# Last part of a four-layer graph network: three of a quad's four batches scaled by a diagonal product on TensorE and one on ScalarE, in place of two and two

## The chip, the cores and the metric

The kernel runs on one core of one Trainium2 chip. The metric is the device time in microseconds. The kernel before takes 3130.37 us, the median of three runs from 3129.48 to 3130.62; the profiled execution has a span of 3128.8 us.

## The reference

Four layers, each a graph operation on x (128 batches, 128 nodes, 256 features), added to x and layer-normalized over the features. The change lies in the end of the last layer. Cut to that part:

```python
x_in = agg.reshape(-1, d)                     # agg = A_hat @ x
h   = relu(batchnorm(x_in @ W1.T + b1, g1, be1))
out = h @ W2.T + b2
out = batchnorm(out, g2, be2)                 # per feature, over all batches and nodes
x   = layernorm(x + out)                      # per node, over the 256 features
```

The second batch norm is a scale and a shift for each of 256 features. They are known only when `h @ W2.T` has been computed for all batches. What remains then is: scale and shift every feature, add x, and normalize each row of 256. All values are float32.

## The kernel before

**Tiling.** The 128 batches go in 32 quads of four (`QB` = 4, `NQ` = 32). For each quad `outs[q]` holds `h @ W2.T` in SBUF with features on the partitions: two chunks of 128 features (`DC` = 2), each 128 partitions x 512 columns, 128 columns (nodes) to a batch. The layer's input x lies with nodes on the partitions: `x3s[q]`, 128 x 1024, 256 columns (features) to a batch. It is loaded from HBM by the SyncE queue into twelve buffers (`load_x3`, L1509), eleven of them ahead of the stage.

So each quad must be turned from features on partitions to nodes on partitions, and scaled and shifted on the way. There are two ways in the kernel, two batches each:

- *The ScalarE way* (batches 0 and 1): `halves` (L1349) scales and shifts in place with one activation for each chunk, where scale and shift are one value for each partition. TensorE then transposes each 128 x 128 block into the PSUM bank `pt[0]` (L1520). VectorE adds the bank to x in SBUF (L1537).
- *The diagonal way* (batches 2 and 3): TensorE multiplies the unscaled block by `diag2`, a diagonal matrix of the scales, which transposes and scales at once, into the bank `pt[1]` (L1528). The shift is added to x by GpSimd (L1525, with `shift_bc`, a row of shifts repeated over the partitions). One more product, of x with the identity, 512 columns wide, adds x into the same bank (L1530). The sum stays in PSUM, and statistics and normalization read it there.

**The row normalization.** `moments(q, half)` (L1533) takes the statistics of two batches on VectorE (two instructions of L1540 and two of L1542); its first half begins with the addition of L1537. ScalarE takes the root (`sd`, L1584). `coefficients(q)` (L1544) makes the factor and the offset of each row with two small VectorE operations (L1547, and L1548, which reads `mvs` and `rs`, both in SBUF, and writes `nm`). `apply(q)` (L1551) is four activations of 256 columns on ScalarE, one for each batch (L1560), from SBUF for batches 0 and 1 and from PSUM for batches 2 and 3. They write into `x3s[q]`, and GpSimd issues the output DMA of the quad (L1566). In the last quad VectorE does two of the four.

**Order.** This part stands under a manual schedule: each engine's queue has the order in which the code issues, and each engine works through its queue in order. The loop at L1571 issues in iteration q:

1. `moments(q, 0)` on VectorE;
2. `scaled(q + 1)` (L1513): ScalarE's `halves`, TensorE's transposes, GpSimd's shift addition, TensorE's diagonal products and identity product;
3. `coefficients(q - 1)` on VectorE and `apply(q - 1)` on ScalarE, with the output DMA on GpSimd;
4. `moments(q, 1)` on VectorE and the root on ScalarE.

So on ScalarE the order is: `halves` of q+1, four applies of q-1, root of q. On VectorE: first half of q, coefficients of q-1, second half of q. On GpSimd: addition of q+1, output DMA of q-1, so that the addition of q+1 stands behind the output DMA of q-2. On TensorE: all of q+1.

**PSUM.** There are eight banks, handed out in turn; a quad takes two. At the start one more is used to make `shift_bc` (L1523).

Of the kernel before, what the change touches and what calls it, by code (L numbers as in the profile page):

```python
# [11 lines left out]
AF = mybir.ActivationFunctionType  # L12
# [14 lines left out]
def gnn_stack(ctx: ExitStack, tc: tile.TileContext, x, adj, w_qv_t, a, w_out_t, src, dst,  # L27
# [14 lines left out]
    nc = tc.nc  # L42
    B, N, D = x.shape
    H, DH = a.shape
    E = src.shape[0]
    P = 128
# [3 lines left out]
    QB = 4  # L50
# [11 lines left out]
    def ctile(shape, name, dtype=F32, pool=const):  # L62
        return pool.tile(shape, dtype, tag=name, name=name)

    def ps(name):
        return psum.tile([P, 512], F32, tag="ps", name=name)
# [6 lines left out]
    ident = ctile([P, P], "ident")  # L73
# [8 lines left out]
    sc2, sh2 = ctile([P, DC], "sc2"), ctile([P, DC], "sh2")  # L82
# [46 lines left out]
    with ExitStack() as phase:  # L129
# [556 lines left out]
        def layer2(k, b, room=None):  # L686
# [84 lines left out]
            pos = [ps("po2").rearrange("p (t d) -> p t d", d=D) for _ in range(2)]  # L771
            yield
            scaled(0)
            v.p4()
            yield
            v.p3()
            po = mix(0)
            scaled(1)
            yield
            mv = norm(0, po)  # L780
# [102 lines left out]
        bias = ctile([P, D], "bias", pool=cst2)  # L883
# [435 lines left out]
    with ExitStack() as phase:  # L1319
# [25 lines left out]
        diag2 = ctile([P, DC, P], "diag2", pool=cst)  # L1345
        shift_bc = ctile([P, D], "shift_bc", pool=cst)
        wide = ctile([P, DC, P], "wide", pool=cst)

        def halves(q, o, ag):  # L1349
            nc.scalar.activation(ag[:, o, :2 * N], ag[:, o, :2 * N], AF.Identity, bias=sh2[:, o:o + 1],  # L1350
                                 scale=sc2[:, o:o + 1])

        def spread(o):
# [3 lines left out]
        with tc.manual_schedule(engines=None):  # L1357
# [112 lines left out]
            def norm_over(o):  # L1470
                batch_norm(st2, o, bn2, sc2, sh2, K3 + o)
                halves(0, o, outs[0])
                spread(o)
# [31 lines left out]
            x3s, sums, mvs, coefs = {}, {}, {}, {}  # L1505
# [7 lines left out]
            def scaled(q):  # L1513
                ag = outs[q]
                pt = [ps("pt3").rearrange("p (b d) -> p b d", d=D) for _ in range(2)]
                for o in range(DC):
                    if q > 0:
                        halves(q, o, ag)
                    for j in range(2):
                        nc.tensor.transpose(pt[0][:, j, o * P:(o + 1) * P], ag[:, o, j * N:(j + 1) * N], ident)  # L1520
                if q == 0:
                    pr = ps("shift_ps")[:, :D]
                    nc.tensor.matmul(pr, ones, wide.rearrange("p o n -> p (o n)"), start=True, stop=True)  # L1523
                    nc.scalar.copy(shift_bc, pr)
                nc.gpsimd.tensor_add(x3s[q][:, 2:, :], x3s[q][:, 2:, :], shift_bc.unsqueeze(1).to_broadcast([P, 2, D]))  # L1525
                for j in range(2):
                    for o in range(DC):
                        nc.tensor.matmul(pt[1][:, j, o * P:(o + 1) * P], ag[:, o, (j + 2) * N:(j + 3) * N], diag2[:, o, :],  # L1528
                                         start=(j == 0 and o == 0), stop=False, skip_group_check=True)
                nc.tensor.matmul(pt[1], ident, x3s[q][:, 2:, :], start=False, stop=True, skip_group_check=True)  # L1530
                sums[q] = pt

            def moments(q, half):  # L1533
                if half == 0:
                    mvs[q] = wk.tile([P, QB, 2], F32, tag="mv3", name="mv3", bufs=3)
                    moments.st = wk.tile([P, QB, 6], F32, tag="st3", name="st3", bufs=2)
                    nc.vector.tensor_add(x3s[q][:, :2, :], x3s[q][:, :2, :], sums[q][0])  # L1537
                src_ = x3s[q][:, :2, :] if half == 0 else sums[q][1]
                for t in range(2):
                    nc.vector.bn_stats(moments.st[:, 2 * half + t, :], src_[:, t, :])  # L1540
                for t in range(2):
                    nc.vector.bn_aggr(mvs[q][:, 2 * half + t, :], moments.st[:, 2 * half + t, :])  # L1542

# [7 lines left out]
            def apply(q):  # L1551
                rs, nm = coefs[q]
                o_q = out[q * QB:(q + 1) * QB].rearrange("b n d -> n b d")
                for i in range(QB):
                    src_ = x3s[q][:, i, :] if i < 2 else sums[q][1][:, i - 2, :]
                    if q == NQ - 1 and i < 2:
                        nc.vector.tensor_scalar(x3s[q][:, i, :], src_, mvs[q][:, i, 0:1], rs[:, i:i + 1],
                                                op0=ALU.subtract, op1=ALU.mult)
                    else:
                        nc.scalar.activation(x3s[q][:, i, :], src_, AF.Identity, bias=nm[:, i:i + 1],  # L1560
                                             scale=rs[:, i:i + 1])
                if q == NQ - 1:
                    nc.sync.dma_start(o_q[:, :2], x3s[q][:, :2, :])
                    nc.scalar.dma_start(o_q[:, 2:], x3s[q][:, 2:, :])
                else:
                    nc.gpsimd.dma_start(o_q, x3s[q])  # L1566

            for q in range(NB - 1):
                load_x3(q)
            scaled(0)  # L1570
            for q in range(NQ + 1):  # L1571
                if q < NQ:
                    moments(q, 0)
                if q + 1 < NQ:
                    scaled(q + 1)
                if q > 0:
                    coefficients(q - 1)
                    apply(q - 1)
                    if q + NB - 2 < NQ:
                        load_x3(q + NB - 2)  # L1580
                if q < NQ:
                    moments(q, 1)
                    sd = wk.tile([P, QB], F32, tag="sd3", name="sd3", bufs=2)
                    nc.scalar.activation(sd, mvs[q][:, :, 1], AF.Sqrt, bias=eps)  # L1584
                    coefs[q] = sd
# [44 lines left out]
```

## Time and profile before

Busy time by stage, from the trace (columns in us; PE is TensorE's matmuls, DVE is VectorE, ACT ScalarE, POOL GpSimd; DMA is the mean busy share of the 16 DMA engines):

| stage, us | length | PE | DVE | ACT | POOL | DMA share |
|---|---|---|---|---|---|---|
| 0 to 2400 | 2400 | 2378.8 | 1793.0 | 993.3 | 504.0 | 0.35 to 0.41 |
| 2400 to 2760 | 360 | 356.5 | 235.1 | 142.6 | 44.7 | 0.04 to 0.29 |
| 2760 to 3014 | 254 | 248.4 | 191.5 | 140.9 | 38.8 | 0.46 |
| 3014 to 3129 | 115 | 92.0 | 97.4 | 99.0 | 64.8 | 0.72 |

The last row is the part described above. An engine's busy time is the union of its instructions' spans; for the matmuls, whose ends are modelled and which overlap, it is an upper limit. The costliest groups of that part are these (mean duration of one instruction; consecutive instructions on ScalarE and TensorE overlap, so their step from start to start is shorter):

| line | engine, what | instructions | mean ns |
|---|---|---|---|
| L1350 | ACT, `halves`, 256 columns | 64 | 619 |
| L1560 | ACT, apply from SBUF, 256 columns | 62 | 617 |
| L1560 | ACT, apply from PSUM, 256 columns | 64 | 579 |
| L1584 | ACT, root | 32 | 318 |
| L1537 | DVE, x plus `pt[0]`, 512 columns | 32 | 687 |
| L1540 | DVE, statistics, 256 columns | 128 | 420 |
| L1548 | DVE, offsets, 4 columns | 32 | 237 |
| L1525 | POOL, shift added to x, 512 columns | 32 | 1279 |
| L1566 | POOL, issue of the output DMA | 31 | 772 |
| L1520 | PE, transposes | 128 | 302 |
| L1528 | PE, diagonal products, two instructions each | 256 | 280 |
| L1530 | PE, identity product, 512 columns, two instructions each | 64 | 640 |

A table like this tells how long each instruction ran, not which of them the end waited for. For that, one reads the busy share in the even part of the stage, and then a timeline of all engines over one period of the loop.

### The profile page before, as it was taken

Reading aid. Unit: us, or ns where it says so; the run is one execution under the profiler, and the core shown is the slowest. Engines: PE = TensorE matmul, PEld = TensorE weight load, DVE = VectorE, ACT = ScalarE, POOL = GpSimd, SP = SyncE. Lnnn points to the kernel's source line nnn. Section 1 sums busy time; section 2 is a strip of 40 time slices with the busy share of each in tenths; the row PEclk is TensorE's granted clock in tenths of the full one; section 3 lists DMA queues with packets and bytes.
Section 4 is the critical chain, followed back from the end, with each engine's and each line's share of the span. In section 5 each row is a group of like instructions: output and inputs, shape, how many; then the busy total and the mean of one; then the engine's idle time right before and its main releaser. Section 6 shows DMA issues by size and latency. Waiting matters only on the chain. (4 is left out here: it accounts for less than half of the span.)

```text
span 3128.8 us, 39836 instructions
## 1 busy us (share of the span) xinstructions
PE 3075.6 (98%) x14800; PEld 2401.8 (77%) x14800; DVE 2316.9 (74%) x4600; ACT 1375.8 (44%) x2548; POOL 652.3 (21%) x536
## 2 busy tenths in 40 slices
PE   8899999999999999999999999999999999999987
PEld 4688888888888888888888888888888887874444
DVE  8777777777777777777777777777777776458888
ACT  3344443444444444434344444444443444326668
POOL 3311112222211111122222211111222220001135
PEclk9999999999999999999999999999999999999999
DMA  5633233333333332333333333323333331005557
GB/s 182 160 102 94 77 94 109 99 104 109 108 102 82 108 96 80 89 108 102 102 109 109 102 89 101 97 78 95 104 102 101 109 108 41 21 27 206 176 193 273
DMA packets 117473, 340.05 MB, mean 109 GB/s; under 512 B 14880, under 2 KB 51616, under 8 KB 108960
## 3 DMA queue, kind: packets, MB, share of 16 engines
q0 software_dynamic: 44688, 148.40, 19.4%
q1 hardware_dynamic: 70832, 188.18, 16.9%
q8 instruction: 118, 1.93, 0.3%
q10 hardware_dynamic: 1760, 0.92, 0.1%
q14 instruction: 75, 0.61, 0.1%
HBM read 252.00 MB, written 85.46 MB: 108 GB/s over the span
## 5 line engine op out<-in xcount | busy, mean ns | idle before, releaser
L580 PE MATMUL ph<-m,w 128*128 128x256 f32 x2048 | 473.1, 379 | 0.0
L660 PE MATMUL p<-w,h 128*128 128x256 f32 x2048 | 462.8, 379 | 0.0
L580 PEld LDWEIGHTS ph<-m,w 128*128 128x128 f32 x2048 | 386.8, 190 | 77.9 <-issue 14.8
L660 PEld LDWEIGHTS p<-w,h 128*128 128x128 f32 x2048 | 388.9, 190 | 66.4 <-issue 7.9
L336 POOL DMA_INDIRECT zs<-qd,src_idx x120 | 116.3, 969 | 1372.6 <-DMA qd<-qt 1338.2
L580 PE MATMUL ph<-m,w_s 128*128 128x256 f32 x1536 | 357.7, 379 | 0.4 <-DVE h L592 0.4
L580 PEld LDWEIGHTS ph<-m,w_s 128*128 128x128 f32 x1536 | 291.7, 190 | 53.6 <-issue 14.8
L336 POOL DMA_INDIRECT zs<-qd,dst_idx x120 | 189.0, 1575 | 332.5 <-DMA zs<-qd,src_idx 323.7
L586 ACT COPY u<-ph 128x512 f32<-128x512 f32 x128 | 74.8, 584 | 354.9 <-PE ph L580 354.9
L418 POOL DMA_INDIRECT attd<-at,att_idx x128 | 141.3, 1104 | 340.3 <-DMA attd<-at,att_idx 252.4
L596 ACT ACTIVATE h<-h 128x512 f32<-128x512 f32 x192 | 121.1, 631 | 138.9 <-DVE h L592 138.9
L113 ACT ACTIVATE ln_sd<-ln_mv,eps 128x2 f32<-128x2 f32 x192 | 55.9, 291 | 276.6 <-DVE ln_mv L108 276.6
L368 DVE SCALAR_TENSOR_TENSOR zs<-zs 128x1024 f32<-128x1024 f32 x125 | 151.4, 1211 | 7.1 <-DMA zs<-qd,dst_idx 5.1
L370 DVE TENSOR_TENSOR zs<-zs,a_bc 128x1024 f32<-128x1024 f32 x125 | 153.1, 1225 | 4.3
L371 DVE TENSOR_REDUCE scores<-zs 128x16 f32<-128x1024 f32 x125 | 152.5, 1220 | 4.3
L723 ACT COPY x2k<-y 128x384 f32<-128x384 f32 x192 | 92.0, 479 | 144.5 <-PE y L716 109.9
L106 DVE BATCH_NORM_STATS2 ln_st<-xr 128x6 f32<-128x256 f32 x384 | 144.6, 419 | 6.6
L121 DVE TENSOR_SCALAR xr<-xr,ln_mv,ln_rs 128x256 f32<-128x256 f32 x384 | 142.8, 414 | 7.0
L592 DVE TENSOR_TENSOR h<-ph,u 128x512 f32<-128x512 f32 x128 | 87.0, 680 | 71.7 <-PE ph L580 54.4
L437 ACT COPY adc<-ad 128x512 f32<-128x512 f32 x125 | 132.9, 1065 | 8.6 <-DMA ad<-attd 8.6
L684 POOL TENSOR_TENSOR xb<-xr,bias 128x512 f32<-128x512 f32 x64 | 99.2, 1549 | 150.7 <-DVE xr L121 143.7
L537 PE MATMUL pm<-wt_t,h 128*128 128x128 f32 x1024 | 126.9, 277 | 0.0
(347 smaller groups left out, 6086.3 us busy)
## 6 DMA issues: line engine op xcount, KB each, us to landing
ad<-attd SPq DMA_DIRECT2D x32, 1024.0 KB, 4.8
zd<-z SPq DMA_DIRECT2D x31, 1024.0 KB, 7.4
zl<-zd SPq DMA_DIRECT2D x62, 512.0 KB, 3.8
xr<-in_x_dram SPq DMA_DIRECT2D x32, 512.0 KB, 7.2
x3d<-xr SPq DMA_DIRECT2D x32, 512.0 KB, 2.6
x3l<-x3d SPq DMA_DIRECT2D x32, 512.0 KB, 5.3
out_dram<-x3l POOLq DMA_DIRECT2D x31, 512.0 KB, 5.7
xg<-in_x_dram SPq DMA_DIRECT2D x29, 512.0 KB, 3.8
```

Of the source, the lines that this page charges most:

```text
L106: nc.vector.bn_stats(st[:, i, :], r[:, i, :])
L121: nc.vector.tensor_scalar(r[:, i, :], r[:, i, :], mv[:, i, 0:1], rs[:, i:i + 1], op0=ALU.subtract, op1=ALU.mult)
L336: nc.gpsimd.indirect_dma_start(out=s.z[c], out_offset=None, in_=s.qd, in_offset=bass.IndirectOffsetOnAxis(ap=idx[:, c:c + 1], axis=0), com ...
L368: nc.vector.scalar_tensor_tensor(z, z, SLOPE, z, op0=ALU.mult, op1=ALU.max)
L370: nc.vector.tensor_mul(z3, z3, a_bc.unsqueeze(1).to_broadcast([P, QB, D]))
L371: nc.vector.reduce_sum(s.es[:, c, :], z.rearrange("p (r d) -> p r d", d=DH), axis=AX.X)
L418: nc.gpsimd.indirect_dma_start(out=ad, out_offset=bass.IndirectOffsetOnAxis(ap=att_idx[:, c:c + 1], axis=0), in_=s.at[:, c, :], in_offset= ...
L437: (copy or nc.scalar.copy)(s.adc[:, j * H:(j + 1) * H, :], s.ad.rearrange("p (s r) -> p r s", r=R)[:, j * H:(j + 1) * H, :])
L537: nc.tensor.matmul(pm[:, c // 2, c % 2, :], quads[k].h1[i, c], wt_t, start=True, stop=True)
L580: nc.tensor.matmul(bank[g][:, i].rearrange("p b n -> p (b n)"), wa[:, c, f:f + P], s.m2[:, blk_b, c].rearrange("p b n -> p (b n)"), start= ...
L596: nc.scalar.activation(h, h if src_ is None else src_, AF.Relu)
L660: nc.tensor.matmul(p3[:, t * D:(t + 1) * D], s.h2[f // 2][:, f % 2, j + t, :], w3_sb[:, f, :], start=(f == 0), stop=(f == K2 - 1))
```

## The change

Batch 1 of each quad moves from the ScalarE way to the diagonal way. `halves` scales batch 0 alone. TensorE transposes one batch and multiplies three by the diagonal matrix; a second identity product, 256 columns wide, adds x for batch 1 into the second half of `pt[0]`. GpSimd adds the shift to three batches instead of two. VectorE's addition covers batch 0 alone; the statistics and the normalization of batch 1 read PSUM. It is meant to take work off ScalarE and VectorE, and to give it to TensorE and GpSimd, which have time left in this part.

```diff
         def halves(q, o, ag):
-            nc.scalar.activation(ag[:, o, :2 * N], ag[:, o, :2 * N], AF.Identity, bias=sh2[:, o:o + 1],
+            nc.scalar.activation(ag[:, o, :N], ag[:, o, :N], AF.Identity, bias=sh2[:, o:o + 1],
                                  scale=sc2[:, o:o + 1])
...
                 for o in range(DC):
                     if q > 0:
                         halves(q, o, ag)
-                    for j in range(2):
-                        nc.tensor.transpose(pt[0][:, j, o * P:(o + 1) * P], ag[:, o, j * N:(j + 1) * N], ident)
+                    nc.tensor.transpose(pt[0][:, 0, o * P:(o + 1) * P], ag[:, o, :N], ident)
...
-                nc.gpsimd.tensor_add(x3s[q][:, 2:, :], x3s[q][:, 2:, :], shift_bc.unsqueeze(1).to_broadcast([P, 2, D]))
-                for j in range(2):
+                nc.gpsimd.tensor_add(x3s[q][:, 1:, :], x3s[q][:, 1:, :], shift_bc.unsqueeze(1).to_broadcast([P, 3, D]))
+                for j in range(1, QB):
                     for o in range(DC):
-                        nc.tensor.matmul(pt[1][:, j, o * P:(o + 1) * P], ag[:, o, (j + 2) * N:(j + 3) * N], diag2[:, o, :],
-                                         start=(j == 0 and o == 0), stop=False, skip_group_check=True)
+                        nc.tensor.matmul(pt[j // 2][:, j % 2, o * P:(o + 1) * P], ag[:, o, j * N:(j + 1) * N],
+                                         diag2[:, o, :], start=(j < 3 and o == 0), stop=False, skip_group_check=True)
+                nc.tensor.matmul(pt[0][:, 1, :], ident, x3s[q][:, 1, :], start=False, stop=True, skip_group_check=True)
                 nc.tensor.matmul(pt[1], ident, x3s[q][:, 2:, :], start=False, stop=True, skip_group_check=True)
...
-                    nc.vector.tensor_add(x3s[q][:, :2, :], x3s[q][:, :2, :], sums[q][0])
-                src_ = x3s[q][:, :2, :] if half == 0 else sums[q][1]
+                    nc.vector.tensor_add(x3s[q][:, 0, :], x3s[q][:, 0, :], sums[q][0][:, 0, :])
                 for t in range(2):
-                    nc.vector.bn_stats(moments.st[:, 2 * half + t, :], src_[:, t, :])
+                    src_ = sums[q][half][:, t, :] if (half, t) != (0, 0) else x3s[q][:, 0, :]
+                    nc.vector.bn_stats(moments.st[:, 2 * half + t, :], src_)
...
-                    src_ = x3s[q][:, i, :] if i < 2 else sums[q][1][:, i - 2, :]
+                    src_ = x3s[q][:, 0, :] if i == 0 else sums[q][i // 2][:, i % 2, :]
```

## The prediction

> **What bounds the kernel now.** I read the busy shares by stage first. Everything the diff touches lies in the last 115 us, from 3014 us on, and only there is TensorE not the full engine. In the even part of that stage ScalarE is busy all the time. Windows view, columns: window, its length, busy time (and instructions) of PE, PEld, DVE, ACT, POOL, then clock, DMA share and GB/s:
>
> ```profile
> 3050.00:3080.00 30.00, 24.53 (x126) 14.69 (x125) 26.96 (x95) 26.99 (x63) 18.06 (x18) 1.00 0.95 324
> 3080.00:3110.00 30.00, 27.76 (x138) 16.09 (x138) 28.06 (x110) 30.00 (x70) 20.47 (x20) 1.00 0.78 281
> ```
>
> ACT has 30.00 of 30.00 us, DVE 28.06, POOL 20.47. So one quad costs what ScalarE needs for it. The timeline of one ordinary quad gives that cost as start-to-start steps (columns: start us, us, engine, line, operation, count, idle before it):
>
> ```profile
> 3055.07 0.33 ACT L1584 ACTIVATE sd<-mv,eps 128x4 f32<-128x4 f32 x1
> ...
> 3055.26 1.12 ACT L1350 ACTIVATE agg<-agg,sh,sc 128x256 f32<-128x256 f32 x2
> 3055.45 0.15 DVE L1547 RECIPROCAL rs<-sd 128x4 f32<-128x4 f32 x1
> 3055.64 0.16 DVE L1548 SCALAR_TENSOR_TENSOR nm<-mv,rs 128x4 f32<-128x4 f32 x1
> 3055.76 0.77 POOL L1566 DMA_DIRECT2D out_dram<-x3l  x1 [0.99 <-POOL x3l L1525]
> ...
> 3056.24 1.12 ACT L1560 ACTIVATE x3l<-x3l,nm,rs 128x256 f32<-128x256 f32 x2
> ...
> 3056.55 1.28 POOL L1525 TENSOR_TENSOR x3l<-x3l,shift_bc 128x512 f32<-128x512 f32 x1
> ...
> 3056.96 0.69 DVE L1537 TENSOR_TENSOR x3l<-x3l,pt 128x512 f32<-128x512 f32 x1
> 3057.22 1.05 ACT L1560 ACTIVATE x3l<-pt,nm,rs 128x256 f32<-128x256 f32 x2
> ...
> 3057.88 1.12 PE L1530 MATMUL pt<-x3l,ident 128*128 128x512 f32 x2
> 3058.12 0.34 ACT L1584 ACTIVATE sd<-mv,eps 128x4 f32<-128x4 f32 x1
> ```
>
> The period is 3058.12 - 3055.07 = 3.05 us: 0.19 for sd, 0.98 for the two scalings (L1350), 0.98 for the two applies from SBUF and 0.90 for the two from PSUM. Call e(n) the end of the last apply of quad n; here e(n) = 3055.21 (the applies of the quad before, 3054.17 + 1.04). GpSimd starts that quad's output DMA 0.55 us after e(n) and the next shift add 1.34 us after it. That add is quad n+3's, by the order of the loop: the add of q+1 stands behind the DMA of q-2.
>
> Then I looked for the quads where ScalarE waits. There are two of 1.5 us among the 29 quads between 3027.6 and 3119.5, both alike; this is one:
>
> ```profile
> 3076.53 1.27 POOL L1525 TENSOR_TENSOR x3l<-x3l,shift_bc 128x512 f32<-128x512 f32 x1
> 3076.54 1.29 DVE L1548 SCALAR_TENSOR_TENSOR nm<-mv,rs 128x4 f32<-128x4 f32 x1
> ...
> 3077.87 1.09 ACT L1560 ACTIVATE x3l<-x3l,nm,rs 128x256 f32<-128x256 f32 x2 [1.50 <-DVE nm L1548]
> ```
>
> The tiny L1548 operation (0.16 us) took 1.29 us: it started with the shift add on GpSimd and ended only when the add did. Normally it starts 0.43 us after e(n), the add at 1.34, so it is ahead by 0.9 us.
>
> **What the Trainium skill says.** "SBUF — State Buffer", section "SBUF: two separate sides": a VectorE operation with two SBUF inputs and a GpSimd operation that reads SBUF exclude each other for the whole instruction; the first to start blocks the other. L1548 reads mv and rs, both in SBUF, and the 1.29 us agrees; L1537 and the statistics have at most one SBUF input, and their rows (0.69 and 0.42 us) never stretch. "ScalarE: Activation LUTs", section "What ACT_TABLE_LOAD costs": an activation takes 0.833 ns per element on top of a fixed part; halving 256 elements should save 0.107 us, and the trace's 0.49 us step becomes 0.39, an estimate. "Perfetto Trace Analysis", section "GPSIMD Engine Instruction": spans on GpSimd are to be timed from start to start; here the add's span is corroborated, since TensorE's L1530 starts 0.05 us after its end.
>
> **The change part by part**, per quad.
> - ScalarE. Two scalings of 128 elements instead of 256: 2 x 0.39, saving 0.20. One apply moves from SBUF (step 0.49) to PSUM (0.45), saving 0.04. ScalarE's own need falls from 3.05 to 2.81 us.
> - VectorE. L1537 covers 256 elements instead of 512. The statistics rows give the slope, 691 - 419 = 272 ns per 256 elements, so 0.69 becomes 0.42. It saves 0.27, but VectorE is not the bound.
> - TensorE. Two transposes become two diagonal products, and a 256-wide identity product is added. Eight instructions of L1528 cover 1.06 us with 0.275 for the last, so steps of 0.11; the four transposes likewise. Minus 2 x 0.11, plus 4 x 0.11, plus about 0.43 (half of 0.86 for a pair of 512): it adds 0.65 to about 2.2, so 2.85 of work. This stays in step with the others.
> - GpSimd. The add grows from 512 to 768 elements. A 512-element add takes 1.28 and a 1024-element subtraction (L1407) 2.35, so the line between them gives 1.81; simple proportion gives 1.92. I take 1.81.
> - The new wait. Batch 1 now ends in pt[0], so pt[0] is complete only after all six diagonal products and the identity product that reads the shifted x3. In the built instruction list of the changed kernel, the statistics of batch 1 carry no wait of their own: L1537's wait on TensorE covers them. So moments(q, 0), which needed nothing but the transposes, now waits for GpSimd's add. Queued behind L1537 on VectorE are all of that half's statistics and then the coefficients of quad q-1 (L1547, L1548), for which ScalarE's applies of q-1 wait.
>
> The new chain from e(n): DMA start 0.55, add 1.34 to 3.15, TensorE 3.20, identity pair 0.65 (two steps of 0.27 and 0.38, the duration of the 256-wide matmuls elsewhere), L1537 at 3.89. From L1537's start to L1548's start was 1.79 us in this timeline (3056.96 to 3058.75); less 0.27, it is 1.52. L1548 thus starts at e(n) + 5.4 instead of 3.5. Then 0.2 to ScalarE, 0.49 + 3 x 0.45 and 0.1 of tail: e(n+2) = e(n) + 7.54. That alone is 3.77 us per quad.
>
> But the next add comes in between. It runs from e(n+1) + 1.34 to + 3.15. With e(n+1) = e(n) + 2.8 to 3.8, L1548 starts at e(n+1) + 1.6 to 2.6, inside the add, and waits for its end. Then e(n+2) = e(n+1) + 3.15 + 0.2 + 1.94 = e(n+1) + 5.29. In the quad after such a long one the chain has had 5.29 us already and VectorE has caught up: L1548 starts 0.55 after e, ahead of the add, and the quad takes ScalarE's 2.81. Then comes a blocked one again. Long and short alternate: (5.29 + 2.81) / 2 = 4.05 us per quad.
>
> The sum: in the 29 quads of the even part, 29 x (4.05 - 3.17), where 3.17 is 91.9 / 29 with the two stalls of before, gives 25.5. The start adds about 1.5: L1537 of quad 0 ran at 3019.0, and now waits for the first add (3020.3 + 1.81) and the identity pair, which moves the first sd from 3023.8 to about 3025.1. The tail is unchanged. Together +27, so 3130.4 + 27 = **3157.5 us**.
>
> **Rivals.**
> - A: the relief of ScalarE is what counts. For it: ACT at 30.00 of 30.00. 29 x 0.24 is 7 and the two stalls 3 more, up to 3120; but the DMA share is 0.95 at 324 GB/s, which leaves little to gain, so about 3123. Against it: the chain above is longer than two periods by 1.4 us from measured pieces alone. Chance 0.06.
> - B: no alternation, because L1548 slips past the add (the identity pair or the DMA start quicker or slower than taken), and the chain rules alone: 29 x (3.77 - 3.17) + 1.5 = 19, about 3149. Chance 0.18.
> - C: the alternation, 3157.5. Chance 0.64.
> - D: the quad after a blocked one is late too (L1548 more than 0.8 us later than I have it), so that every quad takes 5.29: 29 x 2.12 + 1.5 = 63, about 3193. Against it: VectorE has 1.0 us of slack in the long quad. Chance 0.08.
> - E: chain and relief cancel, within 0.2% (3124 to 3137). Chance 0.04.
>
> **How the numbers follow.** The likeliest is C. The range takes in B with some of its spread (a start of the DMA earlier by 0.1 takes 1.5 off) and C with the add at 1.92 (+1.5) and two of the late DMA starts seen in before (0.8 each): 3146 to 3166, leaving out A, D and E, 0.18. Faster 0.06 (A), same 0.04 (E), slower 0.90 (B, C, D).
>
> **What would show it.** In the profile after: L1548 with about half its instances near 1.3 us or more (time from L1548's start to the add's end), L1537 waiting for the 256-wide identity product, ScalarE idle ahead of L1560 and put down to L1548's nm, and ACT busy near 75% between 3030 and 3140. Starts of sd in alternating steps near 5.3 and 2.8 confirm C, even steps of 3.8 confirm B. If ACT stays at 100%, or L1537 starts ahead of the add's end, the new wait isn't there and A holds. The add's mean against 1.81, the two scalings' step against 0.39 and L1537 against 0.42 check the terms.

## The result, and the profile after

The changed kernel takes 3156.41 us (median of four runs, 3155.19 to 3158.24), the kernel before 3129.93 us (four runs, 3128.82 to 3130.62). The ratio is 1.0085, with a 95% interval from 1.0068 to 1.0103: slower by 26.5 us.

The page of the changed kernel has a span of 3153.5 us. The stages ahead of the last part are the same code in every kernel of this study, yet their end differs: the start of the last L93 (the root of the second batch norm, just ahead of the part) lies at 3016.6 us before and at 3013.5 after. So from here on I also give the **part**: from that instruction to the end of the span. It is 3128.8 - 3016.6 = 112.2 us before and 3153.5 - 3013.5 = 140.0 after.

The windows view after, columns as in the prediction:

```profile
3030.00:3060.00 30.00, 24.23 (x138) 17.12 (x137) 21.46 (x88) 21.00 (x52) 18.92 (x16) 1.00 0.75 252
3090.00:3120.00 30.00, 23.66 (x130) 16.38 (x129) 19.62 (x82) 22.41 (x56) 19.30 (x16) 1.00 0.68 234
```

No engine is full any more: ACT fell from 30.00 to 21.0 and 22.4, DVE from 28 to about 20 of 30 us, and the DMA share is 0.68 to 0.75. What sets the time must then be a chain of waits from engine to engine. Two quads of the timeline show it:

```profile
3102.16 0.30 ACT L1584 ACTIVATE sd<-mv,eps 128x4 f32<-128x4 f32 x1
...
3102.69 0.70 PE L1529 MATMUL pt<-x3l,ident 128*128 128x256 f32 x2 [0.54 <-POOL x3l L1524]
3102.82 0.78 POOL L1566 DMA_DIRECT2D out_dram<-x3l  x1 [0.19 <-POOL x3l L1524]
...
3103.42 0.42 DVE L1537 TENSOR_TENSOR x3l<-x3l,pt 128x256 f32<-128x256 f32 x1 [2.47 <-PE pt L1529]
3103.63 1.81 POOL L1524 TENSOR_TENSOR x3l<-x3l,shift_bc 128x768 f32<-128x768 f32 x1
...
3104.95 0.52 DVE L1548 SCALAR_TENSOR_TENSOR nm<-mv,rs 128x4 f32<-128x4 f32 x1
...
3105.51 0.60 ACT L1560 ACTIVATE x3l<-x3l,nm,rs 128x256 f32<-128x256 f32 x1 [2.27 <-DVE nm L1548]
...
3107.36 0.29 ACT L1584 ACTIVATE sd<-mv,eps 128x4 f32<-128x4 f32 x1
...
3107.90 0.16 DVE L1548 SCALAR_TENSOR_TENSOR nm<-mv,rs 128x4 f32<-128x4 f32 x1
3108.01 0.77 POOL L1566 DMA_DIRECT2D out_dram<-x3l  x1 [2.58 <-issue]
...
3108.32 0.59 ACT L1560 ACTIVATE x3l<-x3l,nm,rs 128x256 f32<-128x256 f32 x1
...
3110.16 0.30 ACT L1584 ACTIVATE sd<-mv,eps 128x4 f32<-128x4 f32 x1
```

From sd to sd it is 5.20 and then 2.80 us, and so on to the end. In the long quad VectorE sits idle 2.47 us until the identity product L1529 is done; L1548, too late by then, starts inside the add (3103.63 to 3105.44), is held for 0.52 us instead of 0.16, and ScalarE has waited 2.27 us when it gets nm. In the short quad L1548 comes 0.11 us ahead of the output DMA and ScalarE waits for nothing. L1537 reads batch 0 alone and waits here for the product that writes batch 1's half of the bank. But the statistics of batch 1 stand 0.80 us behind it (3104.22 after 3103.42) and need that product themselves, so of the 2.47 us at most 0.80 can be due to the shared bank; the rest is the order on VectorE. The waits view over 3030 to 3145 us adds them up (waiting line, what it waits for: us in total, times, longest):

```profile
ACT x3l L1560 <- DVE nm L1548: 33.2, 14, 3.1
DVE x3l L1537 <- PE pt L1529: 32.8, 14, 3.3
```

Before, ScalarE waited for nm twice, 3.0 us in all.

### The profile page after: what moved, and what is told of

The parts are those of the page before. It is cut to its first block, busy times and chain, and to the rows that moved or that the text cites. A ratio compares the mean times of both kernels' runs of the same rounds, so it can differ in the third digit from the quotient of the medians.

```text
span 3153.5 us, 40051 instructions
## 1 busy us (share of the span) xinstructions
PE 3088.0 (98%) x14928; PEld 2424.2 (77%) x14928; DVE 2305.7 (73%) x4600; ACT 1369.7 (43%) x2548; POOL 670.1 (21%) x536
```

## The experiments

The theory under test is that of the prediction: (1) the statistics of the first half now wait for the shift add and the identity product, (2) this puts L1548 into the next add, and the two exclude each other (below: the hold). The rival "work" says that the longer add and the additional products cost the time by themselves. The table has the time, its ratio to the kernel before run on the same chip, the part as defined above (of one profile), and the steps from sd to sd in its even stretch. The runs of different chips are compared through these ratios.

| kernel | us | ratio, 95% interval | part, us | steps, us |
|---|---|---|---|---|
| before | 3129.93 | 1 | 112.2 | 3.05, two of 4.7 |
| after | 3156.41 | 1.0085, 1.0068 to 1.0103 | 140.0 | 5.20 / 2.80 |
| e1_swap | 3156.01 | 1.0080, 1.0063 to 1.0097 | 138.4 | 4.68 to 5.46 / 3.06 |
| e2_stats | 3149.31 | 1.0059, 1.0042 to 1.0075 | 130.2 | 5.2 or 4.8 / 2.80, some 3.2 |
| e3_lock | 3150.02 | 1.0063, 1.0046 to 1.0080 | 132.9 | 4.65 / 2.87, later 3.75 |
| e4_add | 3134.43 | 1.0014, 1.0007 to 1.0021 | 113.0 | 3.05, two of 4.9 |
| e5_stats_psum | 3128.53 | 0.9993, 0.9984 to 1.0001 | 111.5 | 2.9 to 3.2, later 3.06, two of 3.7 and 3.8 |
| e6_early_psum | 3126.41 | 0.9990, 0.9981 to 0.9999 | 109.2 | 2.97, later 3.06 |
| e7_before_psum | 3127.96 | 0.9994, 0.9986 to 1.0003 | 110.1 | 3.05, two of 3.6 |
| e9_early | 3143.86 | 1.0048, 1.0032 to 1.0065 | 128.0 | mostly 5.2 / 2.80, some 2.8 more |
| e10_no_ident | 3117.20 | 0.9966, 0.9952 to 0.9980 | 101.4 | 2.80 |
| e11_wait_early | 3140.85 | 1.0042, 1.0026 to 1.0059 | 122.5 | 4.05 / 2.85 |
| e12_vector_add | 3124.71 | 0.9984, 0.9977 to 0.9991 | 107.3 | 3.03 / 2.90 |

**e1_swap: the wait without any of the work.**

```diff
 # the kernel before; the comments on the halves are added here
-                    nc.vector.tensor_add(x3s[q][:, :2, :], x3s[q][:, :2, :], sums[q][0])   # half 0
-                src_ = x3s[q][:, :2, :] if half == 0 else sums[q][1]
+                    nc.vector.tensor_add(x3s[q][:, :2, :], x3s[q][:, :2, :], sums[q][0])   # half 1
+                src_ = x3s[q][:, :2, :] if half == 1 else sums[q][1]
...
```

The slots that the two halves write are exchanged with them.

> The kernel before with the two halves of the statistics exchanged: batches 2 and 3 first, batches 0 and 1 second. No work is added or removed; only the first half, and with it the coefficients of the quad before, now waits for GpSimd's 512-element add and the 512-wide identity product. Theory (wait plus exclusion): L1548 falls to about 4.9 us after e(n), inside the next add, quads alternate between about 4.8 and 3.05 us, 29 x (3.93 - 3.17) = 22, so about 3152 us. Rival without the exclusion (chain alone): 4.89 + 0.2 + 2.0 = 7.1 for two quads, 3.55 each, about 3142 us. Rival 'work' (the longer add and the added products cost the time, the wait is incidental): 3130 us, unchanged.

Measured: 3156.0 us, as slow as the changed kernel, with no instruction more than before and none of another size. Its waits view from 3030 to 3140 us has the same two entries (its L1541 is the statistics, L1549 is L1548):

```profile
DVE st L1541 <- PE pt L1530: 25.8, 14, 2.8
...
ACT x3l L1561 <- DVE nm L1549: 24.1, 14, 2.3
```

So the wait, with the hold that it brings, is enough to cost as much, without any of the added work. That it costs the same to half a microsecond is chance: here ScalarE keeps its 3.05 us and the chain has other pieces. The alternation is there (4.68 and 3.06, expected 4.8 and 3.05), with seven of the long steps 0.2 to 0.8 longer. Of the 4 us above the expected 3152 the start has the most: from the last L93 to the first sd it takes 9.7 us in place of 7.2, which the expectation left out. L1549 was held in nine of the 15 long quads; in the other six it came after the end of the add.

**e4_add: GpSimd's longer work alone.**

```diff
 # the kernel before
...
+                nc.gpsimd.tensor_add(extra, shift_bc[:, :160], shift_bc[:, :160])
                 nc.gpsimd.tensor_add(x3s[q][:, 2:, :], x3s[q][:, 2:, :], shift_bc.unsqueeze(1).to_broadcast([P, 2, D]))
```

> The kernel before with a further add of 160 elements on GpSimd (into a tile that nothing reads) ahead of each shift add, so that GpSimd is held about 1.8 us per quad as in the changed kernel, while all waits stay as before. Theory: there is slack of more than 0.5 us behind the add, so 3129 to 3135 us (a stall or two more or longer). Rival 'work': GpSimd's longer add costs its 0.5 us per quad, about 3145 us.

Measured: 3134.4 us, within the expected 3129 to 3135; runs scatter from 3127.7 to 3142.4. Half a microsecond more on GpSimd in each of 32 quads costs 16 us if it is on the path; it costs about 4. The profiled execution is the fastest of the 18, with a part of 113.0, +0.8, and steps of 3.05 but for two; where a median execution loses its 4 us is not shown.

**e3_lock: the wait without the exclusion.**

```diff
 # the changed kernel
-                nc.vector.scalar_tensor_tensor(nm, mvs[q][:, :, 0], -1.0, rs, op0=ALU.mult, op1=ALU.mult)
+                nc.vector.reciprocal(nm, mvs[q][:, :, 1])
```

> The changed kernel with L1548 replaced by an operation that has one SBUF input (the reciprocal of the variance; the offset of the normalization is left out, so the output is not the reference's). The wait of L1537 stays. Theory: L1548's place never stretches, the alternation goes, the chain alone rules with even steps of about 3.77 us: about 3149 us. Rival 'no part for the exclusion': unchanged, 3156 us, with steps of 2.8 and 5.2.

Measured: 3150.0 us. A pair of quads takes 7.5 us nearly all along, as the chain of the prediction (7.54) has it, against 8.0 with the hold. So taking the hold out of the changed kernel is worth 6.4 us (3156.4 - 3150.0), and the wait alone costs some 20. But the steps are not even as expected: they start as 4.65 and 2.87, and only from about 3080 us on are they 3.71 to 3.79. The alternation thus doesn't need the hold. A chain of the form e(n+2) = e(n) + 7.54 fixes the sum of two steps and leaves open how it is shared between them; that this is why they alternate is argued, not tested.

**e2_stats: all the work, and L1537 freed of the wait.**

```diff
 # the changed kernel: half 0 is batch 0 alone, half 1 the other three
-                    src_ = sums[q][half][:, t, :] if (half, t) != (0, 0) else x3s[q][:, 0, :]
...
+                part = range(1) if half == 0 else range(1, QB)
...
+            def add_x(q):             # issued after moments(q, 0), out of scaled(q)
+                nc.tensor.matmul(pt[0][:, 1, :], ident, x3s[q][:, 1, :], ...)
+                nc.tensor.matmul(pt[1], ident, x3s[q][:, 2:, :], ...)
```

> The changed kernel with all its work, but without the new wait ahead of the coefficients: the first half of the statistics covers batch 0 alone, batch 1 goes to the second half, and the identity products are issued after L1537 of their quad, so that L1537 waits for no add. Theory: L1548 is again some 0.5 us after e(n), ahead of the add; what is left is the second half's chain (add to 3.15, identity pairs to 4.75, statistics and root to 5.9 for two quads), 2.95 to 3.0 us per quad, no alternation: 3122 to 3132 us. Rival 'work': all the added work is still there, so about 3150 to 3157 us.

Measured: 3149.3 us, outside of what the theory said and near what "work" said. The wait at L1537 is gone, as meant, but the timeline shows a hold that I hadn't foreseen:

```profile
3088.53 0.77 POOL L1570 DMA_DIRECT2D out_dram<-x3l  x1 [0.20 <-POOL x3l L1524]
3088.66 2.51 DVE L1552 SCALAR_TENSOR_TENSOR nm<-mv,rs 128x4 f32<-128x4 f32 x1
...
3089.32 1.82 POOL L1524 TENSOR_TENSOR x3l<-x3l,shift_bc 128x768 f32<-128x768 f32 x1
...
3091.20 0.60 ACT L1564 ACTIVATE x3l<-x3l,nm,rs 128x256 f32<-128x256 f32 x1 [2.27 <-DVE nm L1552]
```

L1552 (L1548 in the changed kernel) started 0.66 us ahead of the add, and yet was held to the add's end: 2.51 us. It had started 0.13 us after the output DMA's issue, behind which the add stands. So e2_stats may have lost the wait and kept the hold; e5_stats_psum takes the hold out as well.

**e5_stats_psum, e7_before_psum: e2_stats and the kernel before, with one SBUF input to L1548.** The place of batch 0 in `pt[0]` is free once L1537 has read it:

```diff
+                rp = sums[q][0][:, 0, :QB]
+                nc.vector.reciprocal(rp, coefs[q])
-                nc.vector.scalar_tensor_tensor(nm, mvs[q][:, :, 0], -1.0, rs, op0=ALU.mult, op1=ALU.mult)
+                nc.vector.scalar_tensor_tensor(nm, mvs[q][:, :, 0], -1.0, rp, op0=ALU.mult, op1=ALU.mult)
```

> e2_stats with L1548 made to read only one SBUF input: the reciprocal is computed a second time into the part of pt[0] that batch 0 has left, and L1548 reads it there (0.18 us more on VectorE per quad; nothing is left out). In e2_stats L1548 started 0.1 us after the output DMA's issue on GpSimd and was held until the end of the add behind it. Theory: with one SBUF input it can't be held, so the steps are even, set by the second half's chain: 2.95 to 3.0 us per quad, about 3126 us (3122 to 3131, since the DMA share is near 0.95 at 3.05 us per quad). Rival 'work' (the added products and the longer add hold the stage): still near 3149 us.

> The kernel before with the same second reciprocal into PSUM, L1548 reading one SBUF input. Theory: the two stalls of 1.5 us (L1548 held by the add) go, about 3127 us; but VectorE's 28.06 of 30 us grow by 0.18 per quad to 29.9, so it may come to bound the stage and give the 3 us back: 3126 to 3132 us. If the exclusion were something else than the two SBUF inputs, the two stalls would still be there.

Measured: e5_stats_psum 3128.5 us, 21 us less than e2_stats, by one operand's place. "Work" (3149) is out for good: all the added work is in this kernel, and it is level with the kernel before. L1548 (L1554 here) takes 157 ns in the mean, though with the second reciprocal ahead of it it starts later: 27 of its 32 instances start between 0.12 us after an issue that has an add behind it and the end of that add. One of them:

```profile
3088.70 0.78 POOL L1572 DMA_DIRECT2D out_dram<-x3l  x1 [0.47 <-POOL x3l L1524]
3089.06 0.16 DVE L1554 SCALAR_TENSOR_TENSOR nm<-mv,pt 128x4 f32<-128x4 f32 x1
3089.50 1.83 POOL L1524 TENSOR_TENSOR x3l<-x3l,shift_bc 128x768 f32<-128x768 f32 x1
```

The four kernels make a table of two by two, each against the kernel before on its chip: with neither wait nor hold -1.5 us (e5_stats_psum), with the hold alone +19.2 (e2_stats), with the wait alone +19.9 (e3_lock), with both +26.5 (the changed kernel). Either is enough for some 20 us, and the two overlap, so no fixed share of the 26.5 belongs to one of them.

In the kernel before, e7_before_psum, the two long steps of 4.7 us shrink to 3.6 (late output DMAs remain), and the part from 112.2 to 110.1 us; the ratio's interval, 0.9986 to 1.0003, doesn't separate it from no change.

**e6_early_psum, e9_early: the add one quad earlier, with and without that operand in PSUM.**

```diff
 # e5_stats_psum and e2_stats
-                nc.gpsimd.tensor_add(x3s[q][:, 1:, :], x3s[q][:, 1:, :], shift_bc.unsqueeze(1).to_broadcast([P, 3, D]))
+                for w in (0, 1) if q == 0 else (q + 1,):
+                    if w < NQ:
+                        nc.gpsimd.tensor_add(x3s[w][:, 1:, :], x3s[w][:, 1:, :], shift_bc.unsqueeze(1).to_broadcast([P, 3, D]))
```

> e5_stats_psum with each shift add issued one quad earlier on GpSimd, ahead of the output DMA of q-1 instead of that of q-2's successor, so that the identity products no longer wait for a DMA issue and an add of the same period. Theory: both the wait and the exclusion are gone; what is left is ScalarE's 2.81 and TensorE's 2.85 us per quad, so 29 x (2.85 - 3.17) + 1.5 = -8, about 3122 us, or up to 3128 if the transfers of 1.05 MB per quad can't be had in less than 3.0 us. Rival 'work': 3140 us or more.

> e6_early_psum without the PSUM copy: L1548 reads two SBUF inputs, the add stands one quad earlier. Tells how much of e6's gain the exclusion alone would take. Theory: VectorE no longer waits within the quad, so L1548 starts right behind the root, 0.43 us after e(n) and 0.1 ahead of the output DMA's issue: mostly free, 3121 to 3131 us; if it starts later than the DMA's issue, it is held to the end of the add (2.5 us) every second quad, and 3145 to 3150 us come out as in e2_stats.

Measured: 3126.4 and 3143.9 us; e9_early is near the second of the two cases that were expected for it. With two SBUF inputs L1548 is held again in every second to fifth quad. The end of e9_early has a control that nobody designed: its last two output DMAs have no add behind them. Two lines from there, on GpSimd and VectorE (L1554 is L1548):

```profile
3133.51 0.75 POOL L1572 DMA_DIRECT2D out_dram<-x3l  x1 [2.04 <-ACT sd L1591]
3133.64 0.16 DVE L1554 SCALAR_TENSOR_TENSOR nm<-mv,rs 128x4 f32<-128x4 f32 x1
```

The same 0.13 us after the issue's start, and no hold. In e2_stats the last two issues have no add behind them either, and L1552 starts 0.12 and 0.23 us after theirs and goes free. That points to the add behind the issue as what holds, not to the issue alone, though these are three cases.

In e6_early_psum nothing is held and nobody waits for long, but the quads take 2.97 us and later 3.06, not 2.85. One window of it:

```profile
3080.00:3110.00 30.00, 30.00 (x178) 23.00 (x177) 26.08 (x120) 28.54 (x70) 25.27 (x21) 1.00 0.81 297
```

PE is 30.00 of 30, but the ends of its matmuls are modelled. Its starts in a quad step 0.22 us for the transposes, 1.48 for the twelve diagonal instructions, 0.51 for the 256-wide identity pair, 0.85 for the 512-wide one: 3.06. In e11_wait_early (below) the same twelve take 1.34 and the same pair 0.43:

```profile
3064.72 0.60 PE L1531 MATMUL pt<-x3l,ident 128*128 128x256 f32 x2
3065.15 1.02 PE L1532 MATMUL pt<-x3l,ident 128*128 128x512 f32 x2
...
3066.23 1.50 PE L1529 MATMUL pt<-diag,agg 128*128 128x128 f32 x12
3067.57 0.60 PE L1531 MATMUL pt<-x3l,ident 128*128 128x256 f32 x2
```

So 0.2 us of the 3.06 is not TensorE's work: the pair comes late. In e6_early_psum its weight load starts 0.07 us after the end of VectorE's addition (L1542 there is L1537) in every quad from 3026 us on:

```profile
3086.84 0.42 DVE L1542 TENSOR_TENSOR x3l<-x3l,pt 128x256 f32<-128x256 f32 x1
...
3087.33 0.30 PEld L1535 LDWEIGHTS pt<-x3l,ident 128*128 128x128 f32 x2
3087.36 0.67 PE L1535 MATMUL pt<-x3l,ident 128*128 128x256 f32 x2
...
3087.87 1.02 PE L1536 MATMUL pt<-x3l,ident 128*128 128x512 f32 x2
...
3088.93 0.76 DVE L1546 BATCH_NORM_STATS2 st<-pt 128x6 f32<-128x256 f32 x2 [0.32 <-PE pt L1536]
...
3089.90 0.42 DVE L1542 TENSOR_TENSOR x3l<-x3l,pt 128x256 f32<-128x256 f32 x1
```

That is a loop of two engines: the addition, the identity products issued behind it, the statistics that wait for them, the next addition, 0.52 + 0.51 + 1.06 + 0.97 = 3.06 us. It comes from the order that e2_stats brought in, not from a full TensorE.

**e10_no_ident: is it TensorE, or the transfers?** The 256-wide identity product is left out of e6_early_psum, so x of batch 1 is not added.

> e6_early_psum with the 256-wide identity product left out (x of batch 1 is not added, so the output is not the reference's); nothing else is changed. In e6_early_psum no engine waits for another for long, yet a quad takes 3.06 us; TensorE is busy 30.00 of 30 us and the DMA share is 0.97 while loads last. If TensorE is the bound, a quad loses about 0.4 us of it and falls to ScalarE's 2.8 to 2.95: 29 x -0.15 = -4, about 3121 us, and the steps of sd below 2.95 at least once the loads have ended. If the transfers or GpSimd are the bound, the steps stay at 3.06 and the time at 3126 us.

Measured: 3117.2 us (3121 expected) and steps of 2.80, with ACT at 30.00 of 30:

```profile
3040.00:3070.00 30.00, 29.39 (x174) 20.11 (x175) 28.20 (x129) 30.00 (x76) 27.20 (x22) 1.00 0.98 350
```

So the transfers were not the bound at 3.06: they follow at 350 GB/s to ScalarE's 2.80, which is the relief that the change was made for. Nor was GpSimd, whose work is the same. Between TensorE's own work and the loop above this run doesn't decide, since the product that it leaves out is in both; the steps of e11_wait_early do, for the loop.

**e11_wait_early: how much of the wait is GpSimd's?** The changed kernel with the earlier add and the operand in PSUM, L1537 still waiting for the identity product.

> The changed kernel with L1537's wait left as it is, but each shift add issued one quad earlier on GpSimd and L1548 reading one SBUF input (second reciprocal into PSUM). It takes GpSimd and the exclusion out and leaves what the wait costs on TensorE alone: from e(n), scalings 0.95, transpose and twelve diagonal instructions to 2.55, identity pair to 3.2, then statistics and coefficients (1.52 + 0.18) and applies (2.1): 7.0 for two quads, 3.5 each, even steps, 29 x (3.5 - 3.17) + 1.5 = 11, about 3141 us. If GpSimd's add were the whole of the wait, about 3128 us as in e6_early_psum; if the place of the add made no difference, 3150 us as in e3_lock.

Measured: 3140.9 us, 6.90 us for two quads (7.0 expected), though in steps of 4.05 and 2.85 rather than even ones, again without any hold, as in e3_lock. Each against the kernel before on its chip, e3_lock is 19.9 us slower, e11_wait_early 12.3 slower and e6_early_psum 3.6 faster. So with the hold away, GpSimd's place in the chain is worth some 8 us (10 by the parts in the table), and the products ahead of L1537 on TensorE some 16 (13 by the parts), down to e6_early_psum, where L1537 doesn't wait for them.

**e12_vector_add: a version from these findings.** e11_wait_early without the 256-wide identity product; VectorE adds x for batches 0 and 1 in one operation, as before the change.

```diff
-                nc.tensor.matmul(pt[0][:, 1, :], ident, x3s[q][:, 1, :], start=False, stop=True, skip_group_check=True)
-                    nc.vector.tensor_add(x3s[q][:, 0, :], x3s[q][:, 0, :], sums[q][0][:, 0, :])
+                    nc.vector.tensor_add(x3s[q][:, :2, :], x3s[q][:, :2, :], sums[q][0])
...
```

Statistics and normalization of batch 1 read SBUF again.

> A version meant to beat both: three batches by the diagonal product and the shift add one quad earlier as in e11, L1548 reading one SBUF input, but x of batch 1 added by VectorE together with batch 0's (512 columns, as before the change) instead of by a 256-wide identity product. It takes 0.5 us per quad off TensorE (3.06 in e6_early_psum) and puts 0.27 on VectorE (2.63 per quad in e10_no_ident, of which the second reciprocal is 0.18): VectorE 2.90, ScalarE 2.85, TensorE 2.55. If these hold, 2.9 us per quad, even steps, 29 x (2.9 - 3.17) + 1 = -7, about 3122 us. If the half with L1537 still waits too long for the diagonal product of batch 1, it stays at 3126 to 3130 us.

Measured: 3124.7 us, ratio 0.9984 (0.9977 to 0.9991) to the kernel before; a pair of quads takes 5.93 us. It is faster than both kernels, by 4.6 us of 3129, less than the expected 7. How much of that the third batch has is not shown: no run has the earlier add and the operand in PSUM with two and two batches, and e7_before_psum, with the operand alone, lies at 0.9986 to 1.0003. For it speaks the step of 2.97 us, below the 3.05 that ScalarE needed before: 29 x 0.08 = 2.3 us, an estimate.

## Why the prediction was right, point by point

- **The bound before** (ScalarE, 3.05 us per quad) and its relief to 2.81: e10_no_ident shows 2.80 when nothing else holds. The step of the two scalings was 0.385 us (0.77 for the pair in the timeline after, 3107.55 to 3108.32), estimated 0.39 from the Trainium skill's page "ScalarE: Activation LUTs", section "What ACT_TABLE_LOAD costs", which thus agrees.
- **The new wait**, stated as L1537 behind the add and the identity product: shown by the line of L1537 above and by e1_swap. The places along the chain, from e(n) = 3099.48 in the quad shown: add to 3102.64 (+3.16, predicted 3.15), L1529 +3.21 (3.20), L1537 +3.94 (3.89), L1548 +5.47 (5.4). The add took 1.816 us (1.81), L1537 0.421 (0.42).
- **Rival B**, the chain alone, 3.77 us per quad and 3149 us: e3_lock measured that in the mean, 3.75 and 3150.0, but not its even steps.
- **The alternation**, 5.29 and 2.81: measured 5.20 and 2.80, a pair 0.1 us shorter than predicted (behind a hold ScalarE starts 0.07 us after the add's end, 3105.51 against 3105.44, where the sum had 0.2). From the end of the applies of quad 0 to that of quad 30 it is 3147.07 - 3026.11 = 120.96 us against 3122.34 - 3027.67 = 94.67 before, 26.3 more, where the prediction's even part had 25.5. There is some luck in this: the shorter pairs take 1.4 us off in 14 pairs, and two longer steps (5.73 and 6.05) put 1.4 on. The start cost 1.1 (last L93 to first sd: 7.2 us before, 8.3 after), predicted 1.5.
- **Wrong: the hold as what makes the alternation.** The prediction has even steps of 3.8 as soon as L1548 slips past the add. In e3_lock and e11_wait_early it is never held, and long and short steps alternate in the first half of the one and all through the other. The long step of the sum was still right, since it was worked out from the add's end.
- **Mis-sized: how long L1548 is held.** I wrote that half its instances would last 1.3 us or more. In 12 of the 14 long quads it was near 0.5, one 0.25 and one 1.38. It followed from my own numbers: a start at e(n+1) + 2.6 and an end at + 3.15 leave 0.55. The sum was worked out with those and wasn't touched, but it should have told me that beside the wait the hold adds little (6.4 us).
- **TensorE's need**, 2.85 us per quad, holds by its pieces: in e11_wait_early the twelve diagonal instructions take 1.34 (predicted 1.33) and the 256-wide pair 0.43 (0.43). No run shows TensorE as the bound.
- **Wrong in Rival A: the transfers** as a limit near 3.0 us. They ran at 350 GB/s and 2.80 us per quad in e10_no_ident.
- **Incomplete: when the hold begins.** I took it from the add's start, and called the two stalls of before alike, though in one of them L1548 had started 0.08 us ahead of the add (lines below). e2_stats showed it from the DMA issue in front of it. The short quads of the changed kernel escape by 0.11 us, not by the 0.8 that I worked out, and that the prediction's short step came true rests on this narrow margin: in e2_stats L1548 comes some 0.2 us later against the issue, and the hold costs 20 us.

## What to carry to other kernels

Moving work to engines with time left is priced by what then waits for them, not by their idle share: here no engine was overloaded by the change, and none was full after it. Where an engine works through its queue in order, ask which instruction in it now waits for a later result, and what stands behind that one: e1_swap cost 26 us by the order of two halves alone. And when a small operation on VectorE reads two SBUF tensors near a GpSimd operation, its place in time matters more than its length; here one operand in PSUM ended the holds.

## What the runs showed of the hardware

- The Trainium skill, "SBUF — State Buffer", section "SBUF: two separate sides", says that of a VectorE operation with two SBUF inputs and a GpSimd operation that reads SBUF the first to start keeps the other out for its whole instruction. The runs agree that such an L1548 is held beside an add. By the start times in the trace, though, the first to start isn't always the one that is served. In the kernel before, L1548 started 0.08 us ahead of the add and was held to its end:

```profile
3065.65 1.40 DVE L1548 SCALAR_TENSOR_TENSOR nm<-mv,rs 128x4 f32<-128x4 f32 x1
3065.73 1.28 POOL L1525 TENSOR_TENSOR x3l<-x3l,shift_bc 128x512 f32<-128x512 f32 x1
```

- An add that stands behind a DMA issue on GpSimd holds from about 0.1 us after that issue's start. In e2_stats and e9_early 17 instances of L1548 started 0.12 to 0.36 us after such an issue; 15 took 2.27 to 2.52 us, to the end of the add, and two went free (0.13 and 0.15 us after, both in e2_stats). Of three that started 0.08 to 0.10 us after, all in e9_early, one was held. So the edge is not sharp.
- The hold doesn't always last to the end of the add. In e4_add, where the 160-element add stands behind the issue, L1550 (L1548 there) ended 0.57 us after the issue's start in 23 of the 24 quads in which it started 0.14 to 0.34 us after it, ahead of the add's own start in the trace and at no cost in the steps:

```profile
3086.36 0.78 POOL L1568 DMA_DIRECT2D out_dram<-x3l  x1 [0.58 <-ACT sd L1586]
3086.70 0.23 DVE L1550 SCALAR_TENSOR_TENSOR nm<-mv,rs 128x4 f32<-128x4 f32 x1
3087.16 0.46 POOL L1526 TENSOR_TENSOR wide<-shift_bc 128x160 f32<-128x160 f32 x1
```

With no add behind the issue, four instances that started 0.12 to 0.34 us after it (two in e2_stats, one each in e9_early and e4_add) took 0.16 us. What on GpSimd holds so early is not shown.
- The same operation with one input in PSUM was never held, in six kernels with 32 instances each (157 to 160 ns).
- The code ahead of the last part, the same in all kernels, ended between 3011.1 and 3018.1 us in the profiles. A comparison of effects of a few microseconds needs the part, or many runs.
